# Attention denominators of two images in shared PSUM columns, key sums on ScalarE, new planner costs, and three moved issues in layers 2 and 3

## The chip, the cores and the metric

The kernel runs on one core of a Trainium2 chip. The metric is the device time of one execution in microseconds (us); lower is better. The time before is 3402.57 us, the median of three runs (3402.18 to 3403.87).

## The reference, cut to what matters

The input x has 32 images of 1024 channels and 14 x 14 positions. Two residual layers follow each other, each on a group normalisation of its input. Layer 0 is a chain of three table lookups with softmax scores, each with a batch normalisation; the kernel's code and this text call them layers 1, 2 and 3:

```python
scores = 2.0 * einsum('blcs,cks->blck', v, centroids) - sum(centroids * centroids, -1)
attn = softmax(scores * inv_temp, axis=-1)        # over k = 16
out = einsum('blck,cko->blo', attn, lut)          # then batch norm, relu
```

Layer 1 is a linear attention, the kernel's last stage:

```python
q = elu(q_pre) + 1.0; k = elu(k_pre) + 1.0        # q_pre, k_pre: products with qk_w
km = kh.mean(axis=-1)                             # the mean of the keys over positions
z = 1.0 / (einsum('bhdn,bhd->bhn', qh, km) + 1e-06)
kv = s * s * einsum('bhdn,bhen->bhde', krh, vh)   # krh, qrh: k and q after rope
out = einsum('bhdn,bhde->bhne', qrh, kv) * z[..., None]
attn + lepe                                       # lepe: a 3x3 depthwise convolution of x
```

There are 16 heads of 64 channels. All is float32.

## The kernel before, in words

Everything runs on one core, image pairs at a time (`NP` = 16 pairs, 392 columns each). Layers 1 to 3 are issued in an order written out by hand: each engine takes its instructions in the order of the program, and the framework adds the waits and gives out buffers when the instructions that use them are done.

**Layer 2** (lines 957 to 1077) is a loop of 128 rounds in `units` (line 715), one for each of 8 table blocks of a pair. A round issues scores for four rounds ahead (TensorE, L1024), their exponentials (ScalarE, L565), a transposition on VectorE (L577) and a halving sum on GpSimd (L580) for three ahead, the softmax of two ahead (VectorE L596, L598 and the transposition L608 into a buffer "r", of which there are two; GpSimd's product L615; a total on ScalarE, L619), then DMAs on SP that fill spare rows (L710, L713), then `side2`, and last the table product (TensorE, L731). `side2(60)` builds layer 3's score matrices on VectorE (L382 to L388 and L342 to L356) and calls `biases()`: one TensorE product (L397) and three VectorE operations (L401 to L406). Its operands lie in a tile croom that takes one of the two "r" buffers.

**Layer 3** (from line 1080) works on 14 chunks of 448 columns. `first_chunk` (line 1261) multiplies chunk 0 with eight table column blocks m into PSUM banks, evacuates each with `out(m)` (ScalarE copy L1295, VectorE statistics L1254), and prepares chunk 1 in between: `softmax_steps(1, b, t)` (VectorE, GpSimd, then DMAs that spread rows, L1136 to L1140), `first_sum` (GpSimd, L1210), `weight_sums` (nine GpSimd operations, L1195 to L1197), `weight_differences` (VectorE, L1203) and `other_sums` (VectorE L1216 and L1218, GpSimd L1217). From chunk 1 on, `group(k, n)` does a chunk's products in two halves with seven instead of eight block products (L1355), which need these sums. Before the last chunk, `overflow` (line 626) reduces the softmax totals on VectorE, counts with one TensorE product (L632), and loads the count into a register of all five engines (L635); a branch after the layer reads it.

**Attention** (from line 1475) is a planner, `Plan`. Each piece of work is given to `do` with its engine, a rank, a cost in us and what it reads and writes; `write` plays the pieces in time with these costs and issues them in the order that results, the lowest rank first among those that are ready. The costs change nothing but the order. The pieces concerned, for a pair p:

- `group_norm` (line 1662): averages on TensorE (L1676).
- `channels` (line 1756): for keys and queries, 4 j and 2 r each. `product` is 4 TensorE matmuls (L1767) into one of four PSUM banks "mm"; `relu` and `exp` (ScalarE, L1776 and L1779); `greater` on VectorE. For queries it is one operation of 392 columns (L1784); for keys two of 196 with an accumulator, so that each image's sum over positions comes out too (L1788).
- `rope` on GpSimd (L1811 to L1818), `tokens` (TensorE transpositions L1829, ScalarE copies L1832), `products` (L1866).
- `normalisers` (line 1894): `means` spreads the key sums into the matrices kmm (VectorE, L1899), 32 columns for each j, the first four filled; 16 matmuls (L1917) give the denominators, image i in columns 196 i to 196 i + 196; `inverse` adds 1e-6 (L1926) and takes the reciprocal z (L1927) of 392 columns; a DMA stores z to zd.
- `normalise_q` (line 1938): a DMA spreads zd into zb, GpSimd multiplies (L1952); the last pair selects z with a product (L1949) instead.
- `attend` (TensorE, L1972), `lepe` (VectorE, L1990 and L2004), `side_tap` (ScalarE L2019, GpSimd L2027).

Of the kernel before, what the change touches and what calls it, by code (L numbers as in the profile page):

```python
# [149 lines left out]
def conv_preact_kernel(ctx: ExitStack, tc: tile.TileContext, a: dict, out: bass.AP):  # L150
# [275 lines left out]
    def attention_inputs(stack):  # L426
# [3 lines left out]
        def loads(_):  # L430
            pool = stack.enter_context(tc.tile_pool(name="pre", bufs=1, side="right"))

            def tile_(name, shape):
                given[name] = pool.tile(shape, F32, tag=name, name=name)
                return given[name]

            for n, k in (("qb", a["qb"]), ("kb", a["kb"].rearrange("o (r j p) -> p (o r) j", p=P, r=2))):
                nc.sync.dma_start(tile_(n, [P, 2, 4]), k)
                tile_(n + "u", [P, 2, 4])
                tile_(n + "d", [P, 2, 4])  # L440
            for n, shape in (("lepe_w", [P, CT, 9]), ("lepe_b", [P, CT]), ("kvmask", [P, 256])):
                nc.sync.dma_start(tile_(n, shape), a[n])

            for n in ("cosq", "sinq"):
                t = tile_(n, [P, 4, 14])
                v = a[n].rearrange("p j (r c) -> p j r c", c=14)
                nc.sync.dma_start(t[:, :2], v[:, :2, :, 0])
                nc.sync.dma_start(t[:, 2:], v[:, 2:, 0, :])
            for n, shape in (
                ("hmean", [P, 4]),  # L450
                ("hp", [P, 4, 32]),
                ("hsel", [P, P]),
                ("x1", [P, 4, N2]),
                ("x0", [P, 4, N2]),
                ("o3_0", [P, 2, N2]),
                ("o3_1", [P, 2, N2]),
            ):
                tile_(n, shape)
            for h in (1, 0):
                for i in range(2):  # L460
                    nc.sync.dma_start(
                        given[f"x{h}"][:, :, i * HW : (i + 1) * HW],
                        x[i, 4 * h * P : 4 * (h + 1) * P].rearrange("(c q) n -> q c n", q=P),
                    )

        def tables(scratch):
            g = given

            for n in ("qb", "kb"):
                nc.vector.tensor_scalar(g[n + "u"], g[n], 1.0, None, ALU.add)  # L470
                nc.vector.tensor_scalar(g[n + "d"], g[n], -1.0, None, ALU.mult)

            hmask = g["kvmask"].rearrange("p (h e) -> p h e", e=64)[:, :, 0]
            nc.vector.tensor_scalar(g["hmean"], hmask, 1.0 / HW, None, ALU.mult)

            nc.vector.memset(g["hp"], 0.0)
            nc.vector.tensor_copy(g["hp"][:, :, :4], bc(hmask, 1, 4))

        def heads(scratch):
            g = given  # L480
            ph = scratch(P)
            nc.tensor.transpose(ph, g["hp"].rearrange("p j h -> p (j h)"), ident)
            nc.vector.tensor_copy(g["hsel"], ph)
# [12 lines left out]
    def layers(exact, early=None):  # L496
# [129 lines left out]
        def overflow(pool):  # L626

            good = pool.tile([P, 1], F32, tag="good", name="good")
            nc.vector.tensor_scalar(sums, sums, 1e36, None, ALU.is_le)
            nc.vector.tensor_reduce(good, sums, AX.X, ALU.min)  # L630
            pf = scores(1)[:1]
            nc.tensor.matmul(pf, good, ones[:, :1], start=True, stop=True)  # L632
            bad = pool.tile([1, 1], mybir.dt.int32, tag="bad", name="bad")
            nc.vector.tensor_scalar(bad, pf, -1.0, float(P), ALU.mult, ALU.add)
            return nc.values_load(bad[0:1, 0:1], min_val=0, max_val=P)  # L635
# [321 lines left out]
        with ExitStack() as s:  # L957
# [77 lines left out]
            def side2(i):  # L1035
# [12 lines left out]
                if i == 60:  # L1048
                    bias3, biases = score_biases(ps_tr, big, st, 3, raw[3], P, 2, mask8, 4)
                    parts[3] = score_matrices(big, 3, "", raw[3], mask8), bias3  # L1050
                    biases()
# [28 lines left out]
        with ExitStack() as s:  # L1080
# [180 lines left out]
            def first_chunk():  # L1261
# [40 lines left out]
                for m in range(3):  # L1302
                    bank(m)
                for g in range(1, CT):
                    for m in range(3):
                        product(m, g, start=g == 1)
                bank(3)
                for g in range(1, CT):
                    product(3, g, start=g == 1)
                halves(0)  # L1310
                halves(2)
                out(0)
                for f in softmax_steps(1, 0, nxt):
                    f()
                first_sum(1)
                weight_sums()
                t = score3(1, 1)
# [7 lines left out]
                for f in softmax_steps(1, 1, t):  # L1325
                    f()
                out(4)
                for m in range(5, 8):
                    whole(m)
                    if m == 7:  # L1330
                        weight_differences()
                        other_sums(1)
# [111 lines left out]
            for k in range(1, NCH):  # L1444
                if k + 1 == NCH and not exact:
                    add_up(2, 2 * NCH)
                    again = overflow(once)
                if early:
                    early.pop(0)(scores)
                for n in range(2):  # L1450
                    group(k, n)
# [21 lines left out]
    with ExitStack() as s:  # L1473
# [8 lines left out]
        lw, lb, hmean, sel, cos, sin = (  # L1482
            given[n] for n in ("lepe_w", "lepe_b", "hmean", "hsel", "cosq", "sinq")
        )

# [176 lines left out]
        def group_norm(p, h, rank):  # L1662
# [45 lines left out]
            do(PE, rank, 0.3, average(pm, mean), gst, [pm], lag=0.3)  # L1708
            do(DVE, rank, 0.55, centred, [pm, *gst], [key("gq"), key("nmc")])
            do(PE, rank, 0.3, average(pv, g("gq")), [key("gq")], [pv], lag=0.3)  # L1710
# [45 lines left out]
        def channels(p, keys, j, r, t, sums, rank):  # L1756
# [24 lines left out]
            def greater():  # L1781
                d = t()[:, r]
                if not keys:
                    nc.vector.scalar_tensor_tensor(d, pv(), up, e(), ALU.add, ALU.max)  # L1784
                    return
                for i in range(2):
                    v = image(i)
                    nc.vector.scalar_tensor_tensor(  # L1788
                        d[:, v], pv()[:, v], up, e()[:, v], ALU.add, ALU.max,
# [7 lines left out]
            do(PE, rank, 2.76, product, ys_ + done + need, [pq, *held], lag=0.25)  # L1797
            do(ACT, rank - 20, 0.49, relu, [pq], [e])
            do(ACT, rank - 20, 0.46, exp, [], [e])
            if keys:  # L1800
                do(DVE, rank - 20, 0.86, greater, [pq, e], [(t, r), (sums, r, j)])
            else:
                do(DVE, rank - 20, 0.54, greater, [pq, e], [(t, r)])
# [19 lines left out]
        def tokens(dst, dk, blocks, keys, rank):  # L1823
# [7 lines left out]
            do(PE, rank, 0.5, turn, keys, [pt, (dk[0], "room")], lag=0.25)  # L1831
# [21 lines left out]
        def products(i, jp, kts, vts, rank):  # L1853
# [20 lines left out]
            def scaled():  # L1874
# [10 lines left out]
                1.2,  # L1885
# [8 lines left out]
        def normalisers(p, qs, ks, rank):  # L1894


            def means(i):
                def piece():
                    nc.vector.tensor_tensor(  # L1899
                        kmm[i].rearrange("p r j h -> p (r j) h")[:, :, :4],  # L1900
# [12 lines left out]
            def piece():  # L1913
                for i in range(2):
                    for r in range(2):
                        for j in range(4):
                            nc.tensor.matmul(  # L1917
                                pd()[32 * j : 32 * j + 32, image(i)],
                                kmm[i][:, r, j, :],
                                qs[j]()[:, r, image(i)],  # L1920
                                start=(r == 0),
                                stop=(r == 1),
                            )

            def inverse():
                nc.vector.tensor_scalar(z, pd()[:, :N2], 1e-6, None, ALU.add)  # L1926
                nc.vector.reciprocal(z, z)  # L1927

            def keep():
                nc.sync.dma_start(zd[p % 2], z)  # L1930

            qk = [(q, r) for q in qs for r in range(2)]
            do(PE, rank, 2.3, piece, [*qk, ("kmm", 0), ("kmm", 1)], [pd], lag=0.25)
            do(DVE, rank - 10, 3.1, inverse, [pd], ["z"])
# [3 lines left out]
        def normalise_q(p, n, j, qr, rank):  # L1938
# [6 lines left out]
            def spread():  # L1945
                nc.sync.dma_start(zb(), bc(zd[p % 2, 32 * j : 32 * j + 4], 1, 32))

            def select():
                nc.tensor.matmul(pz()[:, :N2], sel[v], z[v], start=True, stop=True)  # L1949
# [11 lines left out]
        def attend(j, kvs, qr, pa, rank, onto):  # L1961
# [18 lines left out]
            do(PE, rank, 1.57, piece, [kvs[0, j // 2], kvs[1, j // 2], qr], pa, lag=0.25)  # L1980
# [88 lines left out]
        zd = dram.tile([2, P, N2], F32, tag="zd", name="zd")  # L2069
        ru = once.tile([P, 2, N2], F32, tag="ru", name="ru")  # L2070
        z = once.tile([P, N2], F32, tag="z", name="z")
# [186 lines left out]
```

## Time and profile before

| | |
|---|---|
| median of three runs | 3402.57 us |
| the profiled execution | 3404.36 us |
| its span | 3402.6 us |
| layers 1 to 3 | 0 to 2293 us |
| attention | 2293 to 3402.6 us |
| TensorE, VectorE busy | 3311.0 and 2906.9 us |
| GpSimd, ScalarE busy | 2534.4 and 1690.7 us |

In the profile PE is TensorE, PEld its weight loads, DVE VectorE, ACT ScalarE, POOL GpSimd, SP the engine that issues the DMAs. A line such as L1990 is a line of the kernel before. A timeline line gives the start and the duration in us, then the engine, line, operation and operands, and in brackets how long the engine stood idle before and what ended that. A line of stretches gives a stretch's bounds, its length, the busy time of PE, PEld, DVE, ACT and POOL (with the number of instructions in brackets), the clock that TensorE was granted (1.00 is full speed), the busy share of the DMA engines and their GB/s. Matmuls overlap one another, and each float32 matmul of this kernel with a wide weight shows as two records, so costs are taken from one start to the next.

### The profile page before, as it was taken

The numbers are of one execution on the slowest core, as the hardware profiler recorded it, in microseconds if no ns is written. First come the engines' busy times: TensorE is split into PE (matmuls) and PEld (weight loads), VectorE is DVE, ScalarE is ACT, GpSimd is POOL, SyncE is SP. The second block draws the span as 40 slices with busy tenths as digits, with TensorE's granted clock in tenths as the row PEclk, the third lists the DMA queues.
The fourth block names the chain that finished last, engine by engine and source line by source line (L and its number), as shares of the span: only waits on it lengthen the run. The fifth ranks groups of instructions, "written<-read, shape, count | busy, mean of one in ns | idle before, by whom it ended". The sixth has DMA issues, their size and how long they took to land. (4 is left out here: it accounts for less than half of the span.)

```text
span 3402.6 us, 61025 instructions
## 1 busy us (share of the span) xinstructions
PE 3311.0 (97%) x22289; PEld 2021.4 (59%) x22289; DVE 2906.9 (85%) x4555; ACT 1690.7 (50%) x3907; POOL 2534.4 (74%) x1558
## 2 busy tenths in 40 slices
PE   8999999999999999999999999989999999999999
PEld 4555555554445544555478888876666666666665
DVE  8999999996888888888566666656899999999996
ACT  5555555554444434443311111108677777777775
POOL 6999999996888888888332222216988898889887
PEclk9999999999999999999999999999999999999999
DMA  3110111003444434443131111113223333332321
GB/s 119 46 49 28 45 46 46 27 27 99 129 126 124 125 101 124 124 124 90 61 80 38 49 49 49 49 47 133 66 79 90 90 94 94 85 95 79 89 84 46
DMA packets 242252, 267.83 MB, mean 79 GB/s; under 512 B 32812, under 2 KB 239700, under 8 KB 241944
## 3 DMA queue, kind: packets, MB, share of 16 engines
q1 hardware_dynamic: 241248, 263.52, 26.4%
q8 instruction: 179, 2.93, 0.4%
q14 instruction: 129, 1.06, 0.1%
q10 hardware_dynamic: 696, 0.31, 0.0%
HBM read 171.01 MB, written 77.09 MB: 73 GB/s over the span
## 5 line engine op out<-in xcount | busy, mean ns | idle before, releaser
L615 POOL TENSOR_TENSOR t<-t,r 128x1568 f32<-128x1568 f32 (+3 forms) x288 | 961.5, 3339 | 530.6 <-issue 202.1
L731 PE MATMUL po<-t,lut 128*128 128x392 f32 x3840 | 1333.8, 500 | 5.4 <-DMA t<-spare 5.4
L731 PEld LDWEIGHTS po<-t,lut 128*128 128x128 f32 x3840 | 711.4, 190 | 605.2 <-issue 82.7
L1767 PE MATMUL mm<-y,lut 128*128 128x392 f32 x2048 | 713.2, 494 | 4.8 <-DVE k L1788 2.5
L577 DVE STREAM_TRANSPOSE tt<-t 128x1568 f32<-128x1568 f32 (+1 forms) x284 | 517.7, 1823 | 152.1 <-ACT t L565 147.8
L565 ACT ACTIVATE t<-sc,cbias 128x392 f32<-128x392 f32 (+1 forms) x624 | 322.5, 598 | 550.0 <-PE sc L894 183.3
L1990 DVE SCALAR_TENSOR_TENSOR pa<-y,lepe_w,pa 128x406 f32<-128x406 f32 x900 | 537.5, 636 | 11.3 <-PE pa L1972 8.6
L608 DVE STREAM_TRANSPOSE r<-rc 128x1568 f32<-128x1568 f32 (+1 forms) x284 | 520.8, 1834 | 10.4
L1767 PEld LDWEIGHTS mm<-y,lut 128*128 128x128 f32 x2048 | 370.1, 188 | 249.0 <-ACT y L1733 5.1
L580 POOL TENSOR_TENSOR tt<-tt 128x784 f32<-128x784 f32 x256 | 470.7, 1839 | 31.1 <-DVE tt L577 31.1
L565 ACT ACTIVATE t<-sc,room 128x392 f32<-128x392 f32 x512 | 259.0, 589 | 413.3 <-issue 176.9
L1355 PE MATMUL po<-t,lut 128*128 128x224 f32 (+2 forms) x1352 | 315.1, 416 | 1.3 <-DMA o3d<-o 1.3
L596 DVE TENSOR_REDUCE sm<-tt 128x98 f32<-128x784 f32 (+1 forms) x284 | 293.5, 1033 | 1.0 <-POOL tt L580 0.8
L1355 PEld LDWEIGHTS po<-t,lut 128*128 128x128 f32 (+1 forms) x1352 | 235.0, 190 | 64.7 <-issue 62.0
L598 DVE RECIPROCAL rc<-sm 128x98 f32<-128x98 f32 (+1 forms) x284 | 220.1, 775 | 9.8
L619 ACT ACTIVATE sm<-sm 128x98 f32<-128x98 f32 (+1 forms) x284 | 85.4, 301 | 152.3 <-DVE rc L598 152.2
L1620 ACT ACTIVATE w<-x,tb,gn_a 128x196 f32<-128x196 f32 x248 | 128.5, 518 | 54.5 <-DVE tb L1488 29.1
L1733 ACT ACTIVATE y<-x,gb,ga 128x196 f32<-128x196 f32 x256 | 123.3, 543 | 37.4 <-POOL gb L1696 37.2
L1779 ACT ACTIVATE e<-e 128x392 f32<-128x392 f32 x256 | 135.4, 529 | 2.9
L1952 POOL TENSOR_TENSOR qr<-qr,zb 128x784 f32<-128x784 f32 x64 | 118.1, 1856 | 24.8 <-DMA zb<-zd 24.7
L1024 PE MATMUL sc<-patch,room 27*32 27x392 f32 x4096 | 122.9, 505 | 8.3 <-DMA patch<-h1d 8.1
L1355 PE MATMUL po<-x,s 128*128 128x224 f32 x624 | 124.9, 357 | 5.6 <-DVE x L1216 5.6
(213 smaller groups left out, 4403.9 us busy)
## 6 DMA issues: line engine op xcount, KB each, us to landing
patch<-h1d SPq DMA_DIRECT2D x383, 108.5 KB
x<-in_x_dram SPq DMA_DIRECT2D x32, 784.0 KB
o3d<-o SPq DMA_DIRECT2D x56, 448.0 KB
x<-in_x_dram SPq DMA_DIRECT2D x64, 392.0 KB
out_dram<-x SPq DMA_DIRECT2D x64, 392.0 KB
o<-o3d SPq DMA_DIRECT2D x62, 392.0 KB
h1d<-pad SPq DMA_DIRECT2D x96, 225.0 KB
patch<-h1d SPq DMA_DIRECT2D x383, 54.2 KB
```

What stands on the lines that cost most here:

```text
L565: nc.scalar.activation(t[:, j, : sc.shape[1]], sc, AF.Identity if exact else AF.Exp, bias=bias[:, j : j + 1],)
L577: nc.vector.transpose(tt, tf)
L580: nc.gpsimd.tensor_tensor(tv[:, :, :8], tv[:, :, :8], tv[:, :, 8:], ALU.add)
L596: nc.vector.tensor_reduce(sm, tv, AX.X, ALU.add)
L598: nc.vector.reciprocal(rc, sm)
L608: nc.vector.transpose(r, bc(rc, 2, KC))
L615: nc.gpsimd.tensor_tensor(v[:, c], v[:, c], r[:, c], ALU.mult)
L731: nc.tensor.matmul(po[h], luts[b][:, j, h * P : (h + 1) * P], ts[u % len(ts)][:, j, :N2], start=(b == 0 and j == j0), stop=(b == 7 and j = ...
L1355: nc.tensor.matmul(dst, w, x, start=start, stop=stop)
L1767: nc.tensor.matmul(pv(), w[kt][:, m0 : m0 + P], ywin(p, first + kt), start=(kt == 0), stop=(kt == 3),)
L1779: nc.scalar.activation(e(), e(), AF.Exp, scale=-1.0)
L1990: nc.vector.scalar_tensor_tensor(acc, neighbours(p, c, offset(k)), lw[:, c, k : k + 1], acc, ALU.mult, ALU.add,)
```

## The change

It has three parts.

**Attention.** The key sums leave VectorE: `greater` is now one operation of 392 columns for keys too, and a new piece `total` on ScalarE copies each image's half into an unused tile with an accumulator. The denominators of the two images go to the same 196 columns and to different rows: image i's heads fill the columns i, i + 2, ... of kmm, and the matmuls of both images accumulate. The reciprocal therefore works on 196 columns, zd's layout follows, and the last pair's selection is two narrower products for each j with two matrices hsel0 and hsel1, prepared in layer 3.

**Planner costs.** TensorE pieces: channel product 2.76 to 2.65, average 0.30 to 0.42, tokens 0.50 to 0.45, key-value products 1.2 to 1.15, denominators 2.3 to 1.6, attend 1.57 to 1.65. VectorE: keys' maximum 0.86 to 0.54, inverse 3.1 to 1.7. ScalarE: the new total 1.08.

**Layers 2 and 3.** `biases()` of layer 3 is called at round 64 instead of 60. In `first_chunk` the softmax steps of chunk 1, its second scores, `first_sum`, `weight_sums` and `other_sums` are issued earlier. In `overflow` the count is split off and issued after the first half of the last chunk, and the register load after the second.

The diff, cut to its core:

```diff
+                ("hsel0", [P, P]), ("hsel1", [P, P]), ("side", [P, 2]),
...
-            nc.vector.tensor_copy(g["hsel"], ph)
+            for i in range(2):
+                nc.vector.tensor_scalar(g[f"hsel{i}"], ph, g["side"][:, i : i + 1], None, ALU.mult)
...
-            pf = scores(1)[:1]
-            nc.tensor.matmul(pf, good, ones[:, :1], start=True, stop=True)
-            bad = pool.tile([1, 1], mybir.dt.int32, tag="bad", name="bad")
-            nc.vector.tensor_scalar(bad, pf, -1.0, float(P), ALU.mult, ALU.add)
-            return nc.values_load(bad[0:1, 0:1], min_val=0, max_val=P)
+            def count():
+                pf = scores(1)[:1]
+                nc.tensor.matmul(pf, good, ones[:, :1], start=True, stop=True)
+                bad = pool.tile([1, 1], mybir.dt.int32, tag="bad", name="bad")
+                nc.vector.tensor_scalar(bad, pf, -1.0, float(P), ALU.mult, ALU.add)
+                return lambda: nc.values_load(bad[0:1, 0:1], min_val=0, max_val=P)
+            return count
...
-                    biases()
+                    parts["biases3"] = biases
+                if i == 64:
+                    parts["biases3"]()
...
                 for g in range(1, CT):
                     for m in range(3):
                         product(m, g, start=g == 1)
+                t = score3(1, 1)
                 bank(3)
...
+                for f in softmax_steps(1, 1, t):
+                    f()
+                weight_sums()
                 halves(0)
                 halves(2)
                 out(0)
-                for f in softmax_steps(1, 0, nxt):
-                    f()
-                first_sum(1)
-                weight_sums()
-                t = score3(1, 1)
                 out(1)
...
-                for f in softmax_steps(1, 1, t):
-                    f()
+                other_sums(1)
                 out(4)
...
-                        other_sums(1)
...
-                    again = overflow(once)
+                    check = overflow(once)
...
-                for n in range(2):
-                    group(k, n)
+                group(k, 0)
+                if check:
+                    check = check()
+                group(k, 1)
+                if check:
+                    again = check()
...
             def greater():
                 d = t()[:, r]
-                if not keys:
-                    nc.vector.scalar_tensor_tensor(d, pv(), up, e(), ALU.add, ALU.max)
-                    return
+                nc.vector.scalar_tensor_tensor(d, pv(), up, e(), ALU.add, ALU.max)
+
+            def total():
                 for i in range(2):
-                    v = image(i)
-                    nc.vector.scalar_tensor_tensor(
-                        d[:, v], pv()[:, v], up, e()[:, v], ALU.add, ALU.max,
+                    nc.scalar.activation(
+                        unread,
+                        t()[:, r, image(i)],
+                        AF.Copy,
                         accum_out=sums()[:, r, j, i : i + 1],
                     )
...
-            do(PE, rank, 2.76, product, ys_ + done + need, [pq, *held], lag=0.25)
+            do(PE, rank, 2.65, product, ys_ + done + need, [pq, *held], lag=0.25)
...
+            do(DVE, rank - 20, 0.54, greater, [pq, e], [(t, r)])
             if keys:
-                do(DVE, rank - 20, 0.86, greater, [pq, e], [(t, r), (sums, r, j)])
-            else:
-                do(DVE, rank - 20, 0.54, greater, [pq, e], [(t, r)])
+                do(ACT, rank, 1.08, total, [(t, r)], [(sums, r, j)])
...
-                                pd()[32 * j : 32 * j + 32, image(i)],
+                                pd()[32 * j : 32 * j + 32, :HW],
                                 kmm[i][:, r, j, :],
                                 qs[j]()[:, r, image(i)],
-                                start=(r == 0),
-                                stop=(r == 1),
+                                start=(i + r == 0),
+                                stop=(i + r == 2),
...
-                nc.sync.dma_start(zd[p % 2], z)
+                nc.sync.dma_start(zd[p % 2].rearrange("r (i n) -> (r i) n", i=2), z)
...
-                nc.tensor.matmul(pz()[:, :N2], sel[v], z[v], start=True, stop=True)
+                for i in range(2):
+                    nc.tensor.matmul(pz()[:, image(i)], sel[i][v], z[v], start=True, stop=True)
```

In `first_chunk`, `softmax_steps(1, 0, nxt)` and `first_sum(1)` now stand right after the three `bank(m)` calls, ahead of all of its products.

## The prediction

> **What bounds the kernel now.** I read the page first, then the granted clock and busy time by stretches of 66 us, then the waits of TensorE (PE), then the timeline around each step that moves.
>
> ```profile
> PE 3311.0 (97%) x22289; PEld 2021.4 (59%) x22289; DVE 2906.9 (85%) x4555; ACT 1690.7 (50%) x3907; POOL 2534.4 (74%) x1558
> ```
>
> TensorE is the bound nearly everywhere: of 3402.6 us it is idle 91.6. The question is which idle stretches go. Attention (from 2293 us on), three stretches in the middle; the columns are length, then busy us of PE, PEld, DVE, ACT, POOL:
>
> ```profile
> 2696.00:2762.00 66.00, 65.44 (x630) 42.45 (x628) 65.25 (x158) 51.38 (x111) 55.99 (x52) 1.00 0.32 90
> 2762.00:2828.00 66.00, 65.11 (x644) 42.49 (x642) 64.98 (x158) 48.94 (x105) 59.23 (x54) 1.00 0.31 90
> 2894.00:2960.00 66.00, 64.77 (x645) 42.02 (x633) 65.06 (x156) 48.54 (x104) 58.09 (x53) 1.00 0.31 87
> ```
>
> TensorE and VectorE are both 98% full; ScalarE has some 17 us of 66 free. TensorE's waits there, in total us, times, longest:
>
> ```profile
> PE mm L1829 <- ACT kt L1832: 5.3, 10, 0.9
> PE mm L1917 <- DVE q L1784: 4.0, 6, 1.2
> PE pa L1972 <- DVE x L2004: 3.1, 4, 1.3
> ```
>
> With the smaller ones (leaving out 11.1 us at the stage's very start) VectorE ends 13.9 us of them, ScalarE 11.9, GpSimd 0.6. Now the three gaps in layers 2 and 3: timeline of TensorE, start, duration, and in brackets the idle time before.
>
> ```profile
> 1231.36 0.79 PE L397 MATMUL pb<-croom 128*128 128x128 f32 x2 [5.53 <-DMA patch<-h1d]
> 1231.95 6.75 PE L731 MATMUL po<-t,lut 128*128 128x392 f32 x12
> ```
> ```profile
> 1688.00 17.87 PE L1272 MATMUL po<-t,lut 64*128 64x448 f32 x48 [1.10 <-ACT o L1295]
> ...
> 1717.16 4.85 PE L1355 MATMUL po<-x,s 128*128 128x224 f32 x12 [5.58 <-DVE x L1216]
> ```
> ```profile
> 2244.55 0.19 PE L632 MATMUL sc<-ones,good 128*1 128x1 f32 x2 [2.25 <-DVE good L630]
> 2246.08 2.51 PE L1355 MATMUL po<-t,lut 128*128 128x224 f32 x12 [1.34 <-DMA o3d<-o]
> ```
>
> The first two long gaps cost more than their length: the matmuls after them run slow. The number before the last two columns is the granted clock:
>
> ```profile
> 1231.40:1238.60 7.20, 7.20 (x14) 3.86 (x14) 6.79 (x11) 0.00 (x0) 1.83 (x1) 0.59 0.41 106
> ```
> ```profile
> 1717.20:1722.00 4.80, 4.80 (x13) 4.36 (x14) 4.80 (x4) 0.00 (x0) 1.36 (x1) 0.50 0.64 213
> ```
>
> **What the Trainium skill says.** "TensorE: Matmul & The Clock Gate", section What's actually happening: an idle window of about 3.4 us brings TensorE's clock to half, and a busy one brings it back. The trace agrees: 0.59 and 0.50 after gaps of 5.53 and 5.58 us, 1.00 after the third, which a small matmul cuts into 2.25 and 1.34. "SBUF — State Buffer", section SBUF: two separate sides: VectorE and GpSimd lock a shared port pair for a whole instruction. Here a 128x2 operation (L344) took 3.18 us and ended when GpSimd's 3.49 us multiply (L615) did; so VectorE's busy time holds waiting too.
>
> **The change, part by part.**
>
> Layer 2, biases at i == 64. At i == 60 VectorE builds the matrices from 1226.97 on, and TensorE stands before the bias product. A round of 12 matmul records takes 5.02 us from scores to scores elsewhere (1257.64 to 1262.66); this one took 13.74 (1224.89 to 1238.63), so 8.7 is lost. The product (two records, 0.6) still runs four rounds later, its operands long ready: 8.1 is to be had. What may come late instead is VectorE: without TensorE's stop its transposition due at 1228.16 starts after the matrices, about 1232.5, so 4.3 late. Cover: GpSimd's product ends at 1263.46 for a table product at 1269.87, 6.4, less a spare-row DMA (0.6 to issue, about 1.4 to land, as 1693.1 to 1694.5 in layer 3), 4.4. The croom tile also holds one of two "r" buffers four rounds longer; L608 then waits for the previous L615, but it already starts 0.87 after it (1263.46, 1264.33), so this costs at most 0.1 a round. I take 0.5 for both: **-7.6**, bounds -8.1 and -3.
>
> Layer 3, first chunk. The gap at 1711.6 is the chain softmax (1,1), its DMAs on SP, x2 on VectorE. Today this chain starts from scores at 1679.5. Moved: after 42 records (15.1 us from 1656.5) scores (1,1) stand at 1671.7; exponentials 2.2 to 1674.7; VectorE's four steps 2.03+2.02+0.85+2.04 to 1682; GpSimd 4.0 to 1686; six DMAs 4.5 and 1.4 to land, 1692; x2 and x4 by 1694.5, needed at about 1711. The first softmax runs 1659 to 1674 on engines idle then (GpSimd is idle 23.9 us before 1687). GpSimd then has nine weight sums, 12 us, to 1698, and a sum, 1.6, to 1700, needed after 1703. SP's stores of o3d come behind the moved DMAs and nobody waits for them. ScalarE's out(0) now stands behind the total of softmax (1,1), about 1680.3, where TensorE wants its bank at 1680.4: up to 0.6 new. The 1.10 before 1688 goes, since the exponentials no longer precede out(1). Sum: 5.58, 2.4 of slow clock (4.85 against 2.43 for 12 records), 1.10, less 0.6: **-8.5**, bounds -9.1 and -4.
>
> Overflow check. TensorE's 2.25+1.34 = 3.6 goes; the matmul stays, its operands ready. The register loads of five queues come after the last group: VectorE's bn_final, then GpSimd's power and the branch are queued behind a load of 0.73. If it overlaps the last statistics it is free; I charge 0.7: **-2.9**, bounds -3.6 and -1.5.
>
> Attention, VectorE. A key channel is two halves of 0.34 (start to start), a query channel one of 0.53:
>
> ```profile
> 2708.46 0.41 DVE L1788 SCALAR_TENSOR_TENSOR k<-mm,kbu,e 128x196 f32<-128x196 f32 x1
> 2708.80 0.08 DVE L1788 DVE_READ_ACCUMULATOR k<-mm,kbu,e 128x1 f32 x1
> ...
> 2764.92 0.55 DVE L1926 TENSOR_SCALAR z<-mm 128x392 f32<-128x392 f32 x1
> 2765.51 2.60 DVE L1927 RECIPROCAL z<-z 128x392 f32<-128x392 f32 x1
> ```
>
> Keys as one: 8 x 0.15 = 1.2 us a pair. The reciprocal: 0.775 for 98 columns (L598), 2.603 for 392, so 6.2 ns a column and 1.39 for 196; with its add of 0.55 to about 0.35 that saves 1.4. Together 2.6 of 65 us. ScalarE gets 16 sums of 196 columns a pair. No row shows this size; the nearest (L619, 112 columns with accumulator) starts every 0.28 us, 84 more columns at 0.833 ns (the Trainium skill, "ScalarE: Activation LUTs", What ACT_TABLE_LOAD costs; copies of 224 and 448 columns here, 0.35 and 0.53, give 0.81) make 0.35: 5.6 a pair, at most 8.5 if nothing overlaps (0.32 and 0.21 each). ScalarE then has 54 to 57 of 66.
>
> TensorE. The denominators keep their 16 matmuls of 196 columns (32 records in 1.53 us); only their target is shared: zero, bounds -0.1 and +0.3 a pair. The last pair's selection makes 8 narrower products of 4: zero. The halved zd store and smaller z shorten a latency on SP of 1.4 us; GpSimd's 24.7 us of waits for zb gain, but it is not the bound.
>
> The new plan weights reorder everything here. A pair takes 65.9 us (the reciprocals run from 2370.9 to 3359.2, 15 steps). TensorE's own work is 16 x 2.69 + 16 x 0.48 + 4 x 1.0 + 4 x 1.54 + 1.7 + 1.5 = 64.1, so 1.8 a pair, 27 in all, is the most. Of the 13.9 us that VectorE makes TensorE wait I take two thirds away, as its free time grows from 1 to 3.6 us a pair; ScalarE's 11.9 I leave: it is fuller, but its planned cost (1.08 a channel) is above 0.70, so the plan leaves it room. **-9.5**, bounds -24 and +8. In the tail GpSimd's products after 3359 set the end, not z: zero.
>
> Sum: -7.6 - 8.5 - 2.9 - 9.5 = -28.5. The profiled execution took 3404.36 us (span 3402.6 and 1.8 around it), giving 3375.9; the median of the runs is 3402.57, giving **3374**. About 0.2% (6.8 us) is what a measurement of this kernel can tell from no change.
>
> **Rivals.**
> - *ScalarE takes what VectorE gives.* TensorE waits for token copies (kt, kv) instead of sums; for it: ScalarE's copies end nearly half of its waits. Attention 0, the gaps go: 3383. Chance 0.25.
> - *VectorE was the true bound in attention.* Both at 98% speaks for it; against it, named waits come from two engines. TensorE gets within 0.4 us of its own work: -22, 3361. Chance 0.13.
> - *Layer 2 only moves its stall*: VectorE's 4.3 us meets less than 4.4 of cover, TensorE stops over 3.4 us and slows down: 6 given back, 3380. Chance 0.07.
> - *Slower: the new sum blocks ScalarE's queue.* It waits for VectorE's maximum, and behind it stand the relus that free TensorE's four "mm" banks. It decides once each of 8 sums a pair holds the queue 1.7 us beyond its own work: 13.6 and 54 pass 65.9, a pair takes 67.7, attention +28, 3411. Against it: VectorE follows its planned costs closely. Chance 0.05.
>
> The forecast has 0.50. The range, 3360 to 3391, reaches from the second rival to the first with smaller gains in the gaps; it leaves out the slow case and the tails. Faster 0.91, same 0.04, slower 0.05.
>
> **What would show it.** Right: no TensorE gap over 2 us near 1231, 1711 and 2244, clock 1.00 there; L1927 at 1.4 us; 256 more sums on ScalarE at 0.35 a start; pairs 65.2 to 65.4 us apart. Wrong: a TensorE wait for spare rows or L615 after i == 60, ScalarE waiting for L1788's successor by over 1 us each, or the pair distance unchanged at 65.9.

## The result and the profile after

The changed kernel takes 3359.03 us (median of 4 runs, 3358.66 to 3359.25) where the kernel before takes 3403.22 (3402.18 to 3411.99): a ratio of 0.9864, 95% interval 0.9847 to 0.9882. The forecast was 3374 with a range from 3360 to 3391. The sign was right; the gain of 44 us ends 1 us beyond the range and is half as much again as the forecast 28.5.

The profiled execution took 3358.99 us, span 3357.2, so 45.4 less of span than before. Where it went (before, after; the bounds of the stages are the VectorE steps that close layers 2 and 3, L318, and the first record of attention's constants, L1488 and L1507):

| stretch | before | after | difference |
|---|---|---|---|
| up to the end of layer 2 | 1637.1 | 1631.2 | -5.9 |
| layer 3 | 653.7 | 640.0 | -13.7 |
| branch | 5.3 | 5.4 | +0.1 |
| attention | 1106.5 | 1080.6 | -25.9 |

Each column is one execution. The first row has an uncertainty of its own: in the traces of this text the last L318 step of layer 1, up to which no edit touches TensorE's work, comes anywhere between 824.7 and 831.0 us. The last section shows why.

The first line of the page shows what moved between the engines: VectorE 42 us less, ScalarE 97 us more, TensorE 14 us less.

```profile
PE 3296.6 (98%) x22297; PEld 2014.2 (60%) x22297; DVE 2864.6 (85%) x4174; ACT 1787.8 (53%) x4419; POOL 2534.2 (75%) x1558
```

The same three stretches of attention as before the change, from the changed kernel (length, busy PE, PEld, DVE, ACT, POOL, clock):

```profile
2696.00:2762.00 66.00, 65.90 (x635) 42.29 (x637) 63.16 (x135) 55.00 (x140) 57.12 (x53) 1.00 0.29 81
2762.00:2828.00 66.00, 65.75 (x656) 42.98 (x649) 63.81 (x136) 57.95 (x145) 58.99 (x55) 1.00 0.33 97
2894.00:2960.00 66.00, 65.72 (x624) 42.49 (x616) 62.80 (x133) 55.20 (x137) 59.70 (x54) 1.00 0.31 88
```

VectorE is down from 65.1 to 63.3 of 66, ScalarE up from 49.6 to 56.1, and TensorE stands still for 0.2 us where it stood for 0.9. Its waits in all of attention, apart from the one at the start (10.1, before 11.1):

```profile
PE mm L1936 <- DVE q L1802: 4.4, 8, 0.9
PE mm L1695 <- DVE gq L1705: 1.8, 2, 1.0
PE mm L1786 <- DVE k L1802: 1.4, 1, 1.4
PE mm L1848 <- DVE q L1802: 1.1, 3, 0.7
PE mm L1695 <- DVE gst L1658: 0.6, 1, 0.6
PE mm L1848 <- ACT kv L1894: 0.5, 1, 0.5
```

Those ended by VectorE went from 13.9 to 9.3 us, those ended by ScalarE from 11.9 to 0.5. ScalarE got more work and now makes TensorE wait less. That is the line that no term of the forecast explains, and the experiments start from it.

The three gaps of layers 2 and 3, timeline of TensorE. Layer 2: the bias product L397 stands in the row without a wait; the waits that are new are for GpSimd's product and for the spare rows.

```profile
1243.70 5.50 PE L742 MATMUL po<-t,lut 128*128 128x392 f32 x16 [0.91 <-POOL spare L617]
...
1250.01 0.49 PE L397 MATMUL pb<-croom 128*128 128x128 f32 x2
...
1268.66 5.50 PE L742 MATMUL po<-t,lut 128*128 128x392 f32 x16 [0.67 <-DMA t<-spare]
```

Layer 3's first chunk: the gap of 5.58 us is gone. The 24 records of L1368 (L1355 before) with the operands x and s, which the gap used to split into 12 in 2.43 us and 12 slow ones in 4.85, now follow one another in 4.70. A wait of 1.04 for ScalarE's copy takes the place of the 1.10.

```profile
1675.88 23.21 PE L1285 MATMUL po<-t,lut 128*128 128x448 f32 x64 [1.04 <-ACT o L1308]
...
1699.99 2.54 PE L1368 MATMUL po<-t,lut 128*128 128x224 f32 x12
1702.36 4.70 PE L1368 MATMUL po<-x,s 128*128 128x224 f32 x24
```

The overflow check: its product follows the one ahead without a wait, and the next one follows it.

```profile
2246.37 0.19 PE L641 MATMUL sc<-ones,good 128*1 128x1 f32 x2
2246.49 2.54 PE L1368 MATMUL po<-t,lut 128*128 128x224 f32 x12
```

The new operations, VectorE's reciprocal and two of ScalarE's sums:

```profile
2735.22 0.35 DVE L1945 TENSOR_SCALAR z<-mm 128x196 f32<-128x196 f32 x1
2735.60 1.38 DVE L1946 RECIPROCAL z<-z 128x196 f32<-128x196 f32 x1
```
```profile
2748.05 0.37 ACT L1806 ACTIVATE unread<-k 128x196 f32<-128x196 f32 x1 [0.66 <-DVE k L1802]
2748.32 0.19 ACT L1806 ACTIVATION_READ_ACCUMULATOR unread<-k 128x1 f32 x1
2748.54 0.37 ACT L1806 ACTIVATE unread<-k 128x196 f32<-128x196 f32 x1
...
2748.90 0.57 ACT L1795 ACTIVATE e<-mm,kbd 128x392 f32<-128x392 f32 x1
```

The reciprocal with its add takes 1.68 us from 2735.22 to the next operation at 2736.90. A channel's two sums take 0.85 from start to start of the next, 0.43 each: above the 0.35 that was taken, inside the bound of 0.53.

### The profile page after: what moved, and what is told of

Its sections match the earlier page's. It is cut to its first block, busy times and chain, and to the rows that moved or that the text cites. A ratio compares the mean times of both kernels' runs of the same rounds, so it can differ in the third digit from the quotient of the medians.

```text
span 3357.2 us, 61041 instructions
## 1 busy us (share of the span) xinstructions
PE 3296.6 (98%) x22297; PEld 2014.2 (60%) x22297; DVE 2864.6 (85%) x4174; ACT 1787.8 (53%) x4419; POOL 2534.2 (75%) x1558
## 5 line engine op out<-in xcount | busy, mean ns | idle before, releaser
L622 POOL TENSOR_TENSOR t<-t,r 128x1568 f32<-128x1568 f32 (+3 forms) x288 | 961.8, 3340 | 519.7 <-issue 221.2
L1368 PE MATMUL po<-t,lut 128*128 128x224 f32 (+2 forms) x1352 | 313.3, 414 | 0.0
L1368 PEld LDWEIGHTS po<-t,lut 128*128 128x128 f32 (+1 forms) x1352 | 233.4, 189 | 62.9 <-issue 60.6
L1381 DVE TENSOR_TENSOR o<-po,o 128x224 f32<-128x224 f32 (+1 forms) x156 | 81.5, 543 | 56.8 <-PE po L1368 51.9
```

The source lines that it names most:

```text
L622: nc.gpsimd.tensor_tensor(v[:, c], v[:, c], r[:, c], ALU.mult)
L1368: nc.tensor.matmul(dst, w, x, start=start, stop=stop)
```

## The experiments

Times are medians beside the kernel before on the same chip, which took 3404.0 to 3405.8 us in these comparisons. Attention is counted as in the table above.

**Taking attention apart.** The theory at this point: attention's 26 us come from VectorE's freed time and the new costs, in shares to be found. Three kernels divide the change, and a fourth gives the changed kernel VectorE's old work back.

*Costs alone* (the kernel before with only the TensorE numbers of the plan changed; denominators 1.6):

```diff
-            do(PE, rank, 2.76, product, ys_ + done + need, [pq, *held], lag=0.25)
+            do(PE, rank, 2.65, product, ys_ + done + need, [pq, *held], lag=0.25)
...
-            do(PE, rank, 2.3, piece, [*qk, ("kmm", 0), ("kmm", 1)], [pd], lag=0.25)
+            do(PE, rank, 1.6, piece, [*qk, ("kmm", 0), ("kmm", 1)], [pd], lag=0.25)
```

> The kernel before with only TensorE's planner costs changed (2.65, 0.42, 0.45, 1.15, 1.65 and 1.6 for the denominators); every operation stays. Theory order (true TensorE costs keep the order in step, so that TensorE no longer meets ScalarE's copies too early): 12 to 20 us faster than before, near 3386. Theory relief (VectorE was the bound, only less work on it helps): within 5 us of before, 3398 to 3408.

Measured: 3419.69 us, ratio 1.0041 (1.0027 to 1.0054); attention 1117.2. Neither theory had this: the new costs by themselves make attention 10.7 us longer. (The other 4.6 us of this execution lie ahead of attention, where the kernels are the same; the last section has them.) Not all of the 10.7 is waiting. TensorE's busy time grows by 5.0 (1070.4 to 1075.3), and part of that is its clock, which falls after some of the longer waits: these 32 records follow waits of 0.98 and 2.17 us and take 3.04 at clock 0.50, where 32 of the same form take 1.60 at 1.00 further on.

```profile
2571.20 3.04 PE L1972 MATMUL pa<-qr,kv 32*64 32x210 f32 x32
```
```profile
2571.20:2574.20 3.00, 3.00 (x34) 2.22 (x33) 2.65 (x7) 2.89 (x7) 0.54 (x1) 0.50 0.25 85
```

*Operations alone* (key sums on ScalarE and shared denominators, with the new planned costs of VectorE and ScalarE; all TensorE costs old; no moves):

> The kernel before with the key sums on ScalarE and the denominators in shared columns, with their own costs, but with the old costs of all TensorE pieces (2.76, 0.3, 0.5, 1.2, 1.57, 2.3). Theory relief: 18 to 24 us faster, near 3381. Theory order: at most 10 us faster, 3393 or more.

Measured: 3398.31, ratio 0.9975 (0.9966 to 0.9984); attention 1100.7. That lies where the theory of the order put it.

*All of attention's part* (operations and costs, no moves in layers 2 and 3):

> All of the attention part and its costs on the kernel before, none of the three moves in layers 2 and 3. Both theories: 24 us faster than before, near 3379; if the moves and the attention part don't add up, it differs from that by over 4 us.

Measured: 3398.48, ratio 0.9979 (0.9971 to 0.9987); attention 1103.8. This is the surprise, some 19 us above what both theories said. The pieces, ranks and costs given to the planner are those of the changed kernel, and attention is 23 us longer than there.

*The changed kernel with VectorE's old work added back*, unknown to the planner: the keys' maximum in two halves with sums that nobody reads, and a second add and reciprocal.

```diff
+                if not keys:
+                    nc.vector.scalar_tensor_tensor(d, pv(), up, e(), ALU.add, ALU.max)
+                    return
+                for i in range(2):
+                    v = image(i)
+                    nc.vector.scalar_tensor_tensor(
+                        d[:, v], pv()[:, v], up, e()[:, v], ALU.add, ALU.max,
+                        accum_out=idle[:, i : i + 1],
+                    )
...
+                nc.vector.tensor_scalar(z2, pd()[:, :HW], 1e-6, None, ALU.add)
+                nc.vector.reciprocal(z2, z2)
```

> The whole changed kernel in its own planned order, but VectorE does its old amount of work unknown to the planner: the keys' maximum in two halves with an accumulator into an unused tile, and the add and reciprocal of 196 columns twice; 2.8 us of VectorE a pair come back. Theory relief: the gain in attention goes, 18 to 26 us slower than the changed kernel, near 3380. Theory order: 0 to 8 us slower, 3359 to 3367.

Measured: 3393.33, ratio 0.9963 (0.9950 to 0.9977); attention 1112.6, more than either theory had. TensorE's waits for VectorE are 29.5 us where the changed kernel has 9.3; the two largest:

```profile
PE mm L1786 <- DVE k L1807: 7.9, 6, 3.1
PE mm L1944 <- DVE q L1803: 6.8, 9, 1.2
```

So the changed kernel's order does need VectorE's freed time. But freed time and costs together do not make 26 us, as the third kernel shows. Something else differs between it and the changed kernel.

**The order that a build draws.** It is a line of the planner that neither the diff nor the forecast touches. At each step of its clock the planner asks the engines for their next piece, in the order of a Python set of names:

```python
engines = {p[0] for p in self.pieces}      # L90
...
            for e in engines:              # L117
```

Such a set of strings has no fixed order from one build to the next. Two of the engines, VectorE and GpSimd, exclude each other in the plan for pieces marked as locked, so which is asked first decides ties. The same input gives one of two orders of the whole stage. Compared with the order of instructions in the traces, the kernel before, the changed kernel, the costs alone and the padded kernel had drawn *VectorE first*; the operations alone and attention's part without moves had drawn *GpSimd first*. The next four kernels fix the draw by listing the engines; the first three change nothing else in kernels that were seen above, and the fourth is the kernel before with the three moves.

```diff
-        engines = {p[0] for p in self.pieces}
+        engines = ["POOL", "DVE", "ACT", "PE", "SP"]
```

> The changed kernel with one line fixed: where the planner takes the engines as a set of names (line 90), whose order can differ from build to build, they are listed, GpSimd ahead of VectorE. The kernel's own profile shows VectorE taken first where both could start under the shared port. Theory 'the order drawn': the same operations and costs give the order that the attention part alone ran with, attention takes about 1104 us where the changed kernel took 1081, and the kernel about 3382. Rival 'the moves upstream lend attention its gain': attention stays at 1081 and the kernel at 3359.

Measured: 3380.48, ratio 0.9923 (0.9910 to 0.9937); attention 1099.6. The largest waits of TensorE in this kernel's attention, and then in that of attention's part without moves, whose lines are numbered 11 lower:

```profile
PE mm L1786 <- ACT vt L1851: 4.1, 3, 2.2
PE mm L1936 <- DVE q L1802: 4.0, 4, 1.2
PE mm L1848 <- DVE q L1802: 3.4, 7, 0.8
```
```profile
PE mm L1775 <- ACT vt L1840: 4.1, 3, 2.2
PE mm L1925 <- DVE q L1791: 4.0, 4, 1.2
PE mm L1837 <- DVE q L1791: 3.4, 7, 0.8
```

The same waits, the same counts: the draw is what made the two kernels differ. Between the best and the worse draw lie 19 us of the change's 26 in attention.

*Operations alone, VectorE first:*

> The kernel before with the new operations of attention at their own planned costs, TensorE's planned costs old, and VectorE listed ahead of GpSimd in the planner (its earlier run had drawn the other order). Theory 'old costs hide the gain': the planner's own totals for the two orders are 1125.9 and 1122.8, so this order gains nothing over the other: attention 1100 to 1105, the kernel 3398 to 3403. Rival 'VectorE first is the better order whatever the costs': attention about 1080, the kernel about 3378.

Measured: 3403.09, ratio 0.9995 (0.9987 to 1.0003); attention 1105.9. VectorE first is no better order in itself, and with TensorE's old costs the 2.6 us a pair of freed VectorE time are worth nothing in this order: 1106.5 before, 1105.9 with it. In the other order the same operations are worth 14.8 us, as the next kernel shows: 1115.5 before, 1100.7 with them.

*The kernel before, GpSimd first:*

> The kernel before with GpSimd listed ahead of VectorE in the planner, nothing else (its own profile shows the other order). Theory 'the order drawn matters only with the new costs': the planner's totals are 1128.9 and 1129.5, the kernel stays at 3403, plus or minus 6. Rival 'GpSimd first is worse everywhere': attention gets some 23 us longer, the kernel about 3426.

Measured: 3411.75, ratio 1.0023 (1.0016 to 1.0029); attention 1115.5. The kernel before had drawn the better of its two, by some 8 us; neither expectation has this size. (The execution behind the 1115.5 is one of the longer ones, 3416.56 us.)

*The three moves alone, VectorE first:*

> The three moved issues alone (biases of layer 2, softmax of the first chunk of layer 3, overflow check), attention as before with VectorE listed ahead of GpSimd, so in the order that the kernel before ran. By the prediction's terms 7.6 + 8.5 + 2.9 = 19.0 less than before: 3384. By the stages of the changed kernel's trace: layer 2 5.9 less, first chunk 9.1, overflow check 2.8, 17.8 together, and up to 3.5 more if the slow clock at 1848 us and the early weight constants go as they did there: 3382 to 3385. Rival 'attention gives some of it back' (its start moves against the transfers that it begins with): over 3390.

Measured: 3384.75, ratio 0.9938 (0.9924 to 0.9951); attention 1106.5, as before the change. The moves bring 19 us by themselves, and attention gives none of it back.

**Which plan is good.** With the draw fixed at VectorE first, four more kernels change one thing in the changed kernel: one planned cost, or one of the two VectorE savings.

```diff
-            do(PE, rank, 2.65, product, ys_ + done + need, [pq, *held], lag=0.25)
+            do(PE, rank, 2.76, product, ys_ + done + need, [pq, *held], lag=0.25)
```

> The changed kernel, VectorE listed first, with one planned cost put back: TensorE's key and query product 2.76 us instead of 2.65 (its rows start 2.69 us apart). Nothing that runs is different but the order. Theory 'the order is the gain, and it needs a TensorE planned no fuller than it is': the planner's own total rises from 1084.8 to 1115.0, attention takes 1095 to 1115 where it took 1081, the kernel 3373 to 3393. Rival 'the freed VectorE time is the gain, the costs are a detail': attention within 5 us of 1081, the kernel 3359 to 3364.

Measured: 3370.61, ratio 0.9903 (0.9888 to 0.9919); attention 1092.0. What runs is the same work; only its order differs. TensorE's waits are now nearly all for VectorE's query channels:

```profile
PE mm L1936 <- DVE q L1802: 13.0, 14, 1.1
PE mm L1786 <- DVE k L1802: 4.3, 9, 1.0
```

The rival, within 5 us of 1081, is out. The theory has the direction, but its 1095 to 1115 starts 3 us too high; the planner's 1115.0 is too high, as can be expected of a plan with too high a cost.

```diff
-            do(PE, rank, 1.6, piece, [*qk, ("kmm", 0), ("kmm", 1)], [pd], lag=0.25)
+            do(PE, rank, 1.44, piece, [*qk, ("kmm", 0), ("kmm", 1)], [pd], lag=0.25)
```

> The changed kernel, VectorE listed first, with the denominators' planned TensorE cost 1.44 us instead of 1.6 (the trace has 1.53 for the 32 records). The planner's own total falls from 1084.8 to 1078.0. Theory 'the planner's total tells which order is good': attention about 1074, the kernel about 3352, faster than both kernels. Rival 'below some 1081 TensorE's own work is the bound, and what is left is noise': the kernel 3357 to 3361.

Measured: 3355.03, ratio 0.9855 (0.9842 to 0.9869); attention 1075.5, close to the theory's 1074; the kernel lies between the two forecasts. By its profile this beats both kernels; as a whole it stands 4 us under the changed kernel, and the intervals of the two ratios overlap. What is left of waits in attention, between 2300 and 3340 us:

```profile
PE mm L1936 <- DVE q L1802: 3.8, 9, 0.5
PE mm L1848 <- ACT kv L1894: 0.5, 1, 0.5
```

*Key sums on ScalarE without the shared denominators:*

```diff
-                                pd()[32 * j : 32 * j + 32, :HW],
+                                pd()[32 * j : 32 * j + 32, image(i)],
...
-            do(DVE, rank - 10, 1.7, inverse, [pd], ["z"])
+            do(DVE, rank - 10, 3.1, inverse, [pd], ["z"])
```

> The changed kernel, VectorE listed first, without the shared denominators: the key sums on ScalarE, the moves and the new TensorE costs stay, the reciprocal is 392 columns wide again (2.60 us) and planned at 3.1. The planner's total is 1096.2. Theory 'both VectorE savings count and the total tells': attention about 1092 to 1097, the kernel 3370 to 3375. Rival 'the key sums alone bring it, since the reciprocal is one long operation a pair': attention about 1081, the kernel 3359.

Measured: 3375.59, ratio 0.9917 (0.9904 to 0.9931); attention 1096.3, as the theory of the total had it.

*Shared denominators without the key sums:*

```diff
-            do(DVE, rank - 20, 0.54, greater, [pq, e], [(t, r)])
...
+                do(DVE, rank - 20, 0.86, greater, [pq, e], [(t, r), (sums, r, j)])
```

> The changed kernel, VectorE listed first, without the key sums on ScalarE: shared denominators, the moves and the new TensorE costs stay, VectorE makes the key channels in two halves with sums again. The planner's total is 1090.6. Theory 'both VectorE savings count and the total tells': attention about 1086 to 1092, the kernel 3364 to 3370. Rival 'the shared denominators alone bring it': attention about 1081, the kernel 3359. If neither saving can carry the order alone, both this and the kernel with key sums alone stand near the 1117 of the costs alone: the kernel about 3395.

Measured: 3368.47, ratio 0.9889 (0.9874 to 0.9904); attention 1086.7, again as the theory had it. Counted from the costs alone (1117.2), the key sums bring 20.9 us, the shared columns 30.5 and both together 36.6: the two do not add up. Counted from the kernel before (1106.5) they are 10.2, 19.8 and 25.9.

All of attention in one table. "Total" is the planner's own clock at its last piece, with its own costs; "waits" are TensorE's in the trace, apart from the one at the start:

| operations | TensorE costs | asked first | total | attention | waits |
|---|---|---|---|---|---|
| before | old | VectorE | 1128.9 | 1106.5 | 26.4 |
| before | old | GpSimd | 1129.5 | 1115.5 | 31.0 |
| before | new | VectorE | 1110.4 | 1117.2 | 31.0 |
| after | old | VectorE | 1125.9 | 1105.9 | 26.5 |
| after | old | GpSimd | 1122.8 | 1100.7 | 21.4 |
| after | new | GpSimd | 1102.7 | 1099.6 to 1103.8 | 20.4 to 21.5 |
| **after** | **new** | **VectorE** | **1084.8** | **1080.6** | **9.8** |
| after | new, product 2.76 | VectorE | 1115.0 | 1092.0 | 20.1 |
| after | new, denominators 1.44 | VectorE | 1078.0 | 1075.5 | 6.9 |
| key sums only | new | VectorE | 1096.2 | 1096.3 | 17.0 |
| shared columns only | new | VectorE | 1090.6 | 1086.7 | 18.0 |

In the six rows with the product at 2.65 (the new costs, near the traced ones) the total tells the measured time within 7 us and ranks them all. In the five with the product at 2.76 it stands 14 to 23 us above it. Among the old costs it still ranks, but it can't be compared across: 1110.4 by the new costs took longer than 1128.9 by the old.

**Layer 2's new stalls.** The forecast had 0.5 us for what comes late once TensorE no longer stops there; the trace has 3.1 (0.91, and two waits for spare rows of 2.2 together). Two kernels move only the round of the bias product:

```diff
-                if i == 64:
+                if i == 62:
```

> The changed kernel, VectorE listed first, the bias product of layer 2 at i == 62 instead of 64, so the croom tile holds one of the two 'r' buffers for two rounds instead of four. In the changed kernel TensorE waits 3.1 us after round 60, for spare rows and GpSimd. Theory 'the held buffer': the waits fall to 1.6 or less, the layer ends 1.5 us earlier. Rival 'VectorE is late by its 4.5 us of matrices, whatever is held': 2.6 to 3.6 us stay.

Measured: 1.3 us of waits up to the end of the layer, which comes at 1629.7; the kernel 3358.23, ratio 0.9864 (0.9847 to 0.9880).

> The changed kernel, VectorE listed first, the bias product of layer 2 at i == 72 instead of 64: the croom tile holds one of the two 'r' buffers for twelve rounds. Theory 'the held buffer': GpSimd and VectorE stay locked to each other for eight rounds more, TensorE's waits grow from 3.1 to 5 us or more. Rival 'VectorE is late by its matrices': it has caught up before the product, 2 to 3.6 us stay.

Measured: 1.8 us of waits, the layer ends at 1630.6; the kernel 3358.67, ratio 0.9862 (0.9846 to 0.9879). TensorE's waits after 1224 us in layer 2, for rounds 64, 62 and 72:

```profile
PE po L742 <- DMA t<-spare: 2.2, 2, 1.6
PE po L742 <- POOL spare L617: 0.9, 1, 0.9
```
```profile
PE po L742 <- DMA t<-spare: 1.3, 3, 0.7
```
```profile
PE po L742 <- POOL spare L617: 1.0, 1, 1.0
PE po L742 <- DMA t<-spare: 0.8, 1, 0.8
```

Holding the buffer for two rounds halved the waits, as that theory had it, but twelve rounds did not double them, though VectorE then waits for GpSimd's L622 nine times (3.3 us) where it waited three times (1.2). Counted from the scores before the matrices (1224.89 before, then 1224.15, 1224.57 and 1225.03) to the end of the layer, the three kernels are 5.2, 7.1 and 6.6 us shorter than the kernel before: 8.3 to 8.4 less their waits. So the waits are what the layer lacks. Neither theory alone gives all three numbers. What stays open is which late step each single wait goes back to; the size of the matter is 1 to 2 us.

## Why the prediction was right or wrong

**Layer 2, -7.6 forecast, -5.9 in the table, -5.2 from round 60 on.** The other 0.7 came earlier, where no term lies. The mechanism is right: scores of the round after come at 1229.17 instead of 1238.63, and the slow stretch is gone. The term that was mis-sized is the cover: "I take 0.5 for both" is 3.1 in the trace, while the 8.1 to be had was 8.3. The working put VectorE 4.3 us late against 4.4 of cover, a margin of 0.1 that was then priced as if it were wide. The rival in which the stall only moves, with a second slow stretch, didn't come: no wait reaches 2 us, and the clock is 1.00 over the bias product.

**First chunk, -8.5 forecast, -9.1 measured**, from layer 3's start to the scores after the first half of the first group (1730.29 before, 1715.31 after). The 5.58 and the slow clock went as worked out. The small terms were not: a wait of 1.04 for ScalarE's copy remains before L1285, where the forecast took 1.10 out and put up to 0.6 in; the rest of the stretch is some 1 us shorter than worked out, which the lines do not place.

**Overflow check, -2.9 forecast, -2.8 measured.** The 3.6 on TensorE went, and 0.9 came back at the end of the layer, where VectorE stands behind its register load; 0.7 was charged.

**The moves together**: 19.0 forecast, 19 us by the kernel that has only them. Layer 3 gained another 1.7 us that no term had; that was luck, told of below.

**Attention, -9.5 forecast, -25.9 measured.** The parts that were costed by operation are right: the reciprocal 1.38 (forecast 1.39), VectorE 43.5 us less in attention or 2.7 a pair (2.6), the denominators' matmuls unchanged at 21.5 us for 448 records from 2400 to 3300 us in both traces, ScalarE 95.9 us more or 6.0 a pair (5.6). The step that failed is the one from these to TensorE's waits: "Of the 13.9 us that VectorE makes TensorE wait I take two thirds away ... ScalarE's 11.9 I leave". Only a third of VectorE's went and nearly all of ScalarE's. The runs show why such a step can't be made. The waits belong to an order, and the order was about to be remade: freed VectorE time in the old plan gives 0.6 us (VectorE first), the new costs without it lose 10.7 (part of it by the clock), both together gain 25.9. The waits of the trace of before could not tell that; the sentence "The new plan weights reorder everything here" stood in the prediction and was not priced. Of the 25.9, 16.6 are these waits and 1.0 the one at the start; the other 8.2 are TensorE's busy time (1070.4 to 1062.2), with the same matmuls but for the last pair's selection. The clock is not the reason: an estimate from stretches of 5 us, busy time times the missing share of the clock, gives 2.8 us before and 3.6 after. Why the busy time fell stays open.

The rival with VectorE as "the true bound" had nearly the right number, 3361, and 0.4 us over TensorE's own work a pair: the pairs are 64.49 us apart and the own work was worked out as 64.1. That is 21.0 of the 25.9 us, over the 15 steps from the first reciprocal to the last; 3.6 lie ahead of the first and 1.3 after the last, where the forecast had nothing. Its reason is half of the cause. VectorE's time is needed, as the padded kernel shows, and is not enough, as the operations alone with VectorE first show.

The rival in which ScalarE takes what VectorE gives is out: ScalarE ends 0.5 us of waits. The slower one, with the sum blocking ScalarE's queue, is not seen: L1806 waits for VectorE 29 times of 128, 27.4 us in all, and TensorE pays 0.5 us for ScalarE.

The range failed for the attention term. Its bounds of -24 and +8 were stated and the -25.9 lies beyond them, the end of -24 was left to a rival of chance 0.13, and the low end of the range was set at that rival's centre with no room below. And with the other draw the same diff gives 3380 us, well within the range: it was a forecast over two outcomes, some 20 us apart, and didn't know of it. That this build drew the better one was luck. The other would have put attention at 6.9 us less, near the -9.5, but by accident: ScalarE would still end 8.1 us of TensorE's waits and VectorE 11.1, not the 11.9 and the third of 13.9 of the forecast.

## What to carry to other kernels

Where a planner orders the work, a change of costs is a change of the order, and the waits of the old trace don't tell which waits the new order will have: here 26.4 us of them became 9.8, 20.4 or 31.0. Work the planner's own total out for both, once its costs are near the traced ones. Check that the order is a function of the source alone before one run is compared with another; here a set of names moved attention by 19 us where the change moved it by 26, and listing the names fixes it. Where cover exceeds lateness by a tenth of a microsecond, price it as if it were absent.

## What the runs showed of the hardware

TensorE's clock fell in layer 3 after a wait of 0.76 us in some kernels and not in others with the same instructions. The kernel before, timeline and granted clock:

```profile
1847.07 1.01 PE L1108 MATMUL sc<-out,cw 32*128 32x448 f32 x2 [0.76 <-ACT t L565]
1848.01 4.22 PE L1355 MATMUL po<-t,lut 128*128 128x224 f32 x12
```
```profile
1848.00:1852.20 4.20, 4.20 (x14) 3.81 (x14) 0.26 (x1) 1.41 (x3) 0.00 (x0) 0.59 0.22 81
```

The changed kernel runs these 12 records in 2.54 us at clock 1.00; with the bias product at round 62 they take 4.22 at 0.59 again; the kernel before with GpSimd asked first has the wait of 0.76 and not the slow records. The Trainium skill, "TensorE: Matmul & The Clock Gate", section HAM oscillation — how this bites in real kernels, asks for no idle gap above some 3.4 us; a gap of 0.76 is far under that, so here the measurement decides: keeping gaps short did not keep the clock up. Its section What's actually happening calls the window free-running and the effect variable from run to run, with which the coming and going of the 1.7 us agrees. Which of it decides was not tried.

The same comes and goes in layer 1. After waits of 1.68 and some 0.65 us the same 20 matmul records, up to the first table product, take 10.30 us at clock 0.50 in the trace of the costs alone, and 6.33 at 1.00 in that of the kernel before:

```profile
40.03:50.33 10.30, 9.70 (x21) 4.36 (x22) 10.09 (x10) 7.21 (x18) 9.81 (x5) 0.50 0.21 54
```
```profile
39.87:46.20 6.33, 6.33 (x21) 3.03 (x21) 6.23 (x6) 5.52 (x13) 5.86 (x3) 1.00 0.09 28
```

In five of the traces of this text layer 1 ends at 830.5 to 831.0 us (the costs alone, the padded kernel, the kernel before with GpSimd first, the moves alone, the shared columns alone), with the clock at 0.50 between 40 and 46 us, in the others at 824.7 to 826.6. Such 5 us stand in the whole time of an execution, and not in the column for attention, so the experiments are better compared by that column.
